# One PSUM pool for layers 0 and 1, and a pool of its own for layer 1's transposed x

## The chip, the core and the metric

The kernel runs on one core of a Trainium2 chip. The metric is the device time of one execution in microseconds, the median of three runs. The engines are TensorE (PE in the profile, PEld for its weight loads), VectorE (DVE), ScalarE (ACT), GpSimd (POOL) and SyncE (SP, which here only issues DMA transfers). All data are float32.

## The reference

Four residual layers act on x of 64 sequences, 32 positions and 512 features, so 2048 rows. Cut to the two layers that matter here:

```python
# layer 0: a weight per sequence, then a feed-forward part with a routed low-rank part and a layer norm
y = einsum('bsi,boi->bso', x, weight[ids])
h = relu(y @ up_w) ** 2
r = ((y @ fc1_w) @ expert_w) * sum(top_2(y @ gate_w))
x = x + layernorm(h @ down_w + r @ fc2_w) * gamma + beta

# layer 1: gated feed-forward part with a low-rank addition per sequence, then a weighted mix
gate = x @ W_gate.T + 0.5 * (x @ A_gate[ids].T) @ B_gate[ids].T      # 512 -> 1376
up   = x @ W_up.T   + 0.5 * (x @ A_up[ids].T)   @ B_up[ids].T
act  = silu(gate) * up
z    = act @ W_down.T + 0.5 * (act @ A_down[ids].T) @ B_down[ids].T  # 1376 -> 512
x = x + z @ W_base.T + b_base + mix_of_8_low_rank_experts(z)
```

Layer 2 is attention over a paged cache with a routed part behind it, and layer 3 a small mix per sequence with low-rank updates. The kernel runs layer 3 as a tail of layer 2.

## The kernel before

The 2048 rows are 16 tiles of 128. **Layer 0** (`layer0`) takes them in four groups of four tiles. For each group it forms y, transposes it, does the up-projection with a seven-product block scheme (`Up`, L251), and then for each tile (`Tile`) a choice (`choose`: L395, L397, L399), the down product `pd` in L246, and `last`: statistics of `pd` on VectorE (L417, L419, L421), a power on GpSimd (L130), the normalised z on VectorE (L424), times gamma on GpSimd (L425), plus x + beta (L426 on GpSimd, L427 on VectorE), and a store by SyncE (L428).

**Layer 1** (`layer1`) takes the tiles in eight groups of two. `Group.x` transposes two tiles of x on TensorE (L613, tile `xT_ps`) and copies them to `xT` on ScalarE (L614); `x_sums` forms four sums of its blocks on VectorE (L623 to L626); `low` is the first half of the low-rank part (`low_ps`). Then eleven blocks f of 128 features follow (`features`): gate and up together are one 2 x 2 block product, done with seven products `p1` to `p7` (all at L577, tiles `acc_a`, `acc_b`, `acc_c`) in place of eight. For this the weights must first be combined: `sums_of(f)` does four VectorE operations per block (L853 to L856), 44 in all, once, before the blocks of group 0 need them. `p1` and `p2` read the loaded weights alone; `p5`, `p6` and `p7` read sums, and `p4` a block of the up weights that the fourth operation has overwritten. `finish` adds the parts up on VectorE (L714, L738, L741 to L743, L747, L748). Behind a group's blocks stand `low_down` and `down`, and the choice and output of a group are done among the first blocks of the next. On the side GpSimd forms sums of the later layers' weights (`all_sums`, L493 to L496) from blocks that SyncE loads (L102), one set per block in the first blocks of each group.

The order: a scheduler orders the instructions of each engine when the program is built, by what they wait for in memory; only TensorE's order is written down by hand (`c.on_pe`), so that it is the program text's. DMA transfers of SyncE go in one queue (q1). A pool of SBUF or PSUM is a stretch of memory with tiles in it. Pools that are open at the same time lie one behind the other, and pools opened after others have closed lie over them; their tiles then wait for what the older pools still hold.

Layer 0's PSUM pool has eight banks under the tags tr, a, b, c, y0 to y3. Layer 1 opens another eight in its place: tr, lo, and two each of a, b and c. Its SBUF pools stand in this order: `l1_first_halves`, `l1_gathered0` and `1`, `l1_x`, `l1_gate_up` (gate1T, up1T and sums_gate_up, 75 KB of each partition), `l1_weights` (bias rows, cat1, base1T, B1), `l1_down`, `l1_group` (xT, x_sums, low_x, actT and others), `l1_tile`, `l1_sums`. Layer 0's are `l0_first`, `l0_seq_weights`, `l0_transposed_x`, `l0_up`, `l0_weights` (latent, down, fc2, gamma, beta), `l0_x`, `l0_group`, `l0_tile`.

Of the kernel before, what the change touches and what calls it, by code (L numbers as in the profile page):

```python
# [24 lines left out]
F32 = mybir.dt.float32  # L25
# [5 lines left out]
PSUM = bass.MemoryType.PSUM  # L31
DRAM = bass.MemoryType.DRAM

P = 128
B, S, D = 64, 32, 512
NT = B * S // P
SEQ = P // S
KC = D // P
# [109 lines left out]
        return call  # L148


def layer0(c, x_in, x_out):

# [1 line left out]
    tc, nc, a = c.tc, c.nc, c.a  # L156
    INT, LAT, NE = 1024, 256, 8
    G = 4
    N = G * P
    n_sets = a["cond0T"].shape[0]  # L160
    with ExitStack() as ctx:
# [6 lines left out]
        xp = ctx.enter_context(tc.tile_pool(name="l0_x", bufs=2))  # L168
        gp = ctx.enter_context(tc.tile_pool(name="l0_group", bufs=2))
        tp = ctx.enter_context(tc.tile_pool(name="l0_tile", bufs=2))  # L170
        ps = ctx.enter_context(tc.tile_pool(name="l0_psum", bufs=1, space=PSUM))

        def transposed_x(g, k, xT=None):
            if k is None:
# [266 lines left out]
        for g in range(groups):  # L441
            xT = transposed_x(g + 1, None) if 0 < g < groups - 1 else None
# [82 lines left out]
                         sums["out", h][:, k])  # L525


def layer1(c, kp, x_in, x_out, x_biased, sums):

# [2 lines left out]
    tc, nc, a = c.tc, c.nc, c.a  # L534
    G = 2
    N = G * P
# [3 lines left out]
    n_cat = NE * R + NE + 1  # L540
# [3 lines left out]
    with ExitStack() as ctx:  # L544
        rp = ctx.enter_context(tc.tile_pool(name="l1_first_halves", bufs=1))
        aps = [ctx.enter_context(tc.tile_pool(name=f"l1_gathered{i}", bufs=1)) for i in range(2)]
        xp = ctx.enter_context(tc.tile_pool(name="l1_x", bufs=4))
        gup = ctx.enter_context(tc.tile_pool(name="l1_gate_up", bufs=1))
        wp = ctx.enter_context(tc.tile_pool(name="l1_weights", bufs=1))
        wdp = ctx.enter_context(tc.tile_pool(name="l1_down", bufs=AHEAD))  # L550
        gp = ctx.enter_context(tc.tile_pool(name="l1_group", bufs=1))
        tp = ctx.enter_context(tc.tile_pool(name="l1_tile", bufs=2))
        sum_p = ctx.enter_context(tc.tile_pool(name="l1_sums", bufs=1))
        ps = ctx.enter_context(tc.tile_pool(name="l1_psum", bufs=1, space=PSUM))


        ids = c.load(kp, "ids1", [P, NT // G], a["ids1"], I32)
# [21 lines left out]
        class Group:  # L579
# [27 lines left out]

            def x(self, t, tag="tr"):
                if t == 0:
                    self.xT = gp.tile([P, KC, N], F32, name="xT")  # L610
                pt = ps.tile([P, KC, P], F32, tag=tag, name="xT_ps")
                for k in range(KC):
                    c.on_pe(nc.tensor.transpose(pt[:, k, :], self.xs[t][:, k * P:(k + 1) * P], c.ident))  # L613
                nc.scalar.copy(self.xT[:, :, t * P:(t + 1) * P], pt)  # L614
                nc.gpsimd.tensor_tensor(self.xs[t], self.xs[t], bias, ALU.add)
# [22 lines left out]

            def low(self):
                n = N // SEQ  # L640
                pt = ps.tile([P, 2, n], F32, tag="lo", name="low_ps")
                for u in range(2):
                    for k in range(KC):
                        for j in range(SEQ):
                            q = slice(2 * R * j, 2 * R * (j + 1))
                            product(pt[q, u, :], self.pair("x", u * KC + k, j),
                                    self.xT[:, k, j * n:(j + 1) * n], k == 0, k == KC - 1)
                self.low_x = gp.tile([P, 2, P], F32, name="low_x")
                self.masked(self.low_x, pt, own_half)

            def low_down(self):
                n = N // SEQ
                pt = ps.tile([P, 1, n], F32, tag="c", bufs=2, name="low_d_ps")
                for f, (_, w) in enumerate(FC):
                    for j in range(SEQ):
                        q = slice(2 * R * j, 2 * R * (j + 1))
                        product(pt[q, 0, :], self.pair("down", f, j)[:w],
                                self.actT[:w, f, j * n:(j + 1) * n], f == 0, f == NFC - 1)
                self.low_d = gp.tile([P, 1, N], F32, name="low_d")
                self.masked(self.low_d, pt, own)  # L660
# [8 lines left out]
            def begin(self, f):  # L669

                if f == 0:
                    self.actT = gp.tile([P, NFC, N], F32, name="actT")
                self.a[f] = ps.tile([P, D], F32, tag="a", bufs=2, name="acc_a")
                self.b[f] = ps.tile([P, D], F32, tag="b", bufs=2, name="acc_b")
                self.c[f] = ps.tile([P, D], F32, tag="c", bufs=2, name="acc_c")
                self.part[f] = {}

            def kept(self, f, name, src):
# [78 lines left out]

            def down(self, fs, last):
                if 0 in fs:
                    self.pz = [ps.tile([P, 2, N], F32, tag=tag, bufs=2, name="pz") for tag in "ab"]  # L760
                for f in fs:
                    w, wd = FC[f][1], self.wd.pop(0)
                    for m in range(KC):
                        product(self.pz[m // 2][:, m % 2, :], wd[:w, m * P:(m + 1) * P],
                                self.actT[:w, f, :], m % 2 == 0 and f == 0, False)
                    self.next_down(f + AHEAD)
                if not last:
                    return
                for m in range(KC):
                    product(self.pz[m // 2][:, m % 2, :], self.B["Bd1"][:, m * P:(m + 1) * P],  # L770
                            self.low_d[:, 0, :], False, m % 2 == 1)
                self.zT = gp.tile([P, KC, N], F32, name="zT")
                nc.scalar.copy(self.zT[:, 0:2, :], self.pz[0])
                nc.vector.tensor_copy(self.zT[:, 2:4, :], self.pz[1])

            def choose(self, t):

                q = slice(t * P, (t + 1) * P)
                ph = ps.tile([P, n_cat], F32, tag="lo", name="ph")
                for k in range(KC):  # L780
                    product(ph, self.zT[:, k, q], wcat[:, k, :], k == 0, k == KC - 1)
                h = tp.tile([P, n_cat], F32, name="h")
                nc.scalar.copy(h, ph)
                logits = h[:, NE * R:NE * R + NE]
                nm = tp.tile([P, 1], F32, name="nm")
                nc.vector.tensor_reduce(nm, logits, AX.X, ALU.max, negate=True)
                e = tp.tile([P, NE], F32, name="e")
                den = tp.tile([P, 2], F32, name="den")
                nc.scalar.activation(e, logits, AF.Exp, bias=nm, accum_out=den[:, 0:1])
                nc.scalar.activation(den[:, 1:2], h[:, n_cat - 1:n_cat], AF.Exp, bias=nb_thr,  # L790
                                     scale=-1.0)
                self.h[t] = h, e, den
# [17 lines left out]
                                        e.unsqueeze(2).to_broadcast([P, NE, R]), ALU.mult)  # L810

            def base(self, t, tag="tr"):
                self.po[t] = ps.tile([P, D], F32, tag=tag, bufs=2 if tag == "a" else 1, name="po")
                for k in range(KC):
                    product(self.po[t], self.zT[:, k, t * P:(t + 1) * P], wbase[:, k, :], k == 0, False)

            def turn(self, t):
                pt = ps.tile([P, P], F32, tag="lo", name="hwT_ps")
                c.on_pe(nc.tensor.transpose(pt, self.h[t].rearrange("p e r -> p (e r)"), c.ident))
                self.h[t] = tp.tile([P, P], F32, name="hwT")  # L820
                nc.scalar.copy(self.h[t], pt)
# [1190 lines left out]
def emit(tc, a, layers=(0, 1, 2)):  # L2012
    with ExitStack() as ctx:
        c = Common(ctx, tc, a)
        dram = ctx.enter_context(tc.tile_pool(name="scratch", bufs=1, space=DRAM))

        def scratch(name):
            tiles = [dram.tile([P, D], F32, name=f"{name}_{t}") for t in range(NT)]
            return lambda t: tiles[t]

        def rows(name):
            return lambda t: a[name][t * P:(t + 1) * P, :]

        x = rows("x")
        for n in layers:
            out = rows("out") if n == layers[-1] else scratch(f"x{n}")
            if n == 0:
                layer0(c, x, out)
            if n != 0 and n == next(m for m in layers if m):
                kp = ctx.enter_context(tc.tile_pool(name="known", bufs=1))  # L2030
                last = Tail(c)
                last.numbers(kp)
                known = Known(c, kp)
                sums = {}
                for h in range(HALVES):
                    sums["in", h] = dram.tile([P, GB, 4, KC // 2, D], F32, name=f"in_sums{h}")
                    sums["out", h] = dram.tile([P, HQP // 2, 4, D // 2], F32, name=f"out_sums{h}")
            if n == 1:
                x_biased = scratch("x_biased")
                layer1(c, kp, x, out, x_biased, sums)  # L2040
            elif n == 2:
                y_part, y = scratch("y_part"), scratch("y")
                attention(c, known, x, y_part, y, sums, last.between(x_biased, y, out))
            x = out
# [87 lines left out]
```

## Time and profile before

| | |
|---|---|
| median of three runs | 3472.89 us (3469.66 to 3475.73) |
| the profiled execution | 3470.0 us, span 3468.2 us from first to last instruction |
| granted TensorE clock, mean | 0.996 |
| busy: PE, DVE, ACT, POOL | 98%, 63%, 47%, 48% of the span |
| layer 0's last product on TensorE ends | 358.26 us |
| layer 1's first product begins | 361.04 us |
| PE busy from 300 to 450 us | 143.94 of 150 us |

How to read the lines: in a timeline the columns are start, duration (of a merged row: of the stretch), engine, line of the kernel, operation, tile written and tiles read, shapes, count, and in brackets the idle time before it with what ended it. In a list of waits they are the total, the number of waits and the longest. In the windows each engine's busy time stands with its number of instructions, then the granted TensorE clock as a share of full speed, the busy share of the DMA engines, and GB/s. A TensorE product in float32 is shown as two matmul records.

### The profile page before, as it was taken

How to read it: one execution, taken by the hardware profiler on the slowest of the kernel's cores; microseconds unless marked ns; L12 is line 12 of the kernel's file. 1: busy time of each engine (PE TensorE's matmuls, PEld its weight loads, DVE VectorE, ACT ScalarE, POOL GpSimd, SP SyncE). 2: the span in 40 equal slices, each digit the busy share in tenths (PEclk: the TensorE clock that was granted, in tenths of full speed). 3: DMA queues.
4: the chain of work that ended last, by engine and by line, in shares of the span. 5: the costliest groups of instructions: out<-in, count | busy, mean ns of one | idle time of the engine just before them, and what ended most of it. 6: DMA issues, size and time to landing. Idle time of an engine off the chain costs nothing. (4 is left out here: it accounts for less than half of the span.)

```text
span 3468.2 us, 66995 instructions
## 1 busy us (share of the span) xinstructions
PE 3412.8 (98%) x21124; PEld 2681.2 (77%) x21124; DVE 2189.0 (63%) x5429; ACT 1627.3 (47%) x4259; POOL 1653.6 (48%) x1650
## 2 busy tenths in 40 slices
PE   8999999999999999999999999999999999999999
PEld 6556788888857778777787777777877778778778
DVE  5454434334458677766767667677676776767467
ACT  6332222222226555555555555555555555656422
POOL 0112433333346655645556455565564655645233
PEclk9999999999999999999999999999999999999999
DMA  5013555545466788887888888878778888887731
GB/s 210 25 52 125 185 161 169 166 158 164 143 219 213 237 264 253 258 261 249 255 257 255 257 257 259 260 250 269 249 255 265 256 269 258 259 255 236 228 114 62
DMA packets 631937, 740.28 MB, mean 213 GB/s; under 512 B 64546, under 2 KB 480290, under 8 KB 631586
## 3 DMA queue, kind: packets, MB, share of 16 engines
q1 hardware_dynamic: 580130, 562.94, 52.1%
q0 software_dynamic: 51456, 173.05, 14.3%
q8 instruction: 172, 2.82, 0.3%
q14 instruction: 179, 1.47, 0.1%
HBM read 689.61 MB, written 46.14 MB: 212 GB/s over the span
## 5 line engine op out<-in xcount | busy, mean ns | idle before, releaser
L1086 POOL DMA_INDIRECT vt<-in_v_rows,v_rows x512 | 516.8, 1009 | 301.3 <-PE po L1060 176.1
L1349 ACT ACTIVATE pr<-pr,low 128x544 f32<-128x544 f32 x512 | 383.3, 749 | 548.0 <-DVE low L1347 546.0
L1342 PE MATMUL sc<-kt,qT 128*128 128x288 f32 (+1 forms) x2048 | 555.3, 394 | 9.1 <-DVE low L1347 5.9
L1342 PEld LDWEIGHTS sc<-kt,qT 128*128 128x128 f32 x2048 | 384.8, 190 | 224.3 <-issue 121.5
L1060 PEld LDWEIGHTS po<-prT,vt 128*128 128x128 f32 x4096 | 523.0, 192 | 33.4 <-ACT prT L1360 13.9
L1060 PE MATMUL po<-prT,vt 128*128 128x128 f32 x4096 | 544.7, 276 | 3.4 <-ACT prT L1360 1.9
L1347 DVE CUSTOM_DVE_ANT_0 pr<-sc,mask 128x544 f32<-128x544 f32 x512 | 368.1, 719 | 141.2 <-PE sc L1342 140.6
L1134 POOL TENSOR_TENSOR projected<-projected,swapped 128x512 f32<-128x512 f32 x160 | 208.3, 1302 | 302.1 <-DVE projected L1133 278.2
L1354 DVE TENSOR_SCALAR pr<-pr,low 128x512 f32<-128x512 f32 x512 | 317.8, 621 | 12.8
L1055 PE MATMUL prT_ps<-ident,pr 128*128 128x128 f32 x2048 | 312.1, 275 | 1.5 <-DVE pr L1354 1.3
L1360 ACT COPY prT<-prT_ps 128x512 f32<-128x512 f32 x512 | 294.0, 574 | 32.3 <-PE prT_ps L1055 24.7
L1351 DVE RECIPROCAL low<-low 128x1 f32<-128x1 f32 x512 | 81.9, 160 | 318.4 <-ACT pr L1349 317.7
L1055 PEld LDWEIGHTS prT_ps<-ident,pr 128*128 128x128 f32 x2048 | 237.7, 142 | 10.8 <-issue 2.8
L1060 PE MATMUL py<-wo,oT 128*128 128x256 f32 x1024 | 242.8, 380 | 0.0
L1060 PE MATMUL pq<-wp,x_sums 128*128 128x512 f32 x512 | 240.5, 593 | 0.1
L1060 PEld LDWEIGHTS py<-wo,oT 128*128 128x128 f32 x1024 | 187.4, 191 | 21.5
L130 POOL TENSOR_TENSOR rs<-rs,minus_half 128x4 f32<-128x4 f32 x160 | 180.1, 1125 | 22.2 <-DVE low L1351 14.6
L1060 PE MATMUL pq<-wp,xT 128*128 128x512 f32 x384 | 182.4, 598 | 5.0 <-DVE projected L1220 5.0
L1352 ACT ACTIVATE own_pr<-pr,low 128x32 f32<-128x32 f32 x512 | 164.8, 322 | 44.1 <-DVE low L1351 41.0
L1060 PE MATMUL py<-wo,o_sum 128*128 128x256 f32 x768 | 182.7, 382 | 2.1 <-DVE o_sum L1278 2.1
L1093 ACT COPY own_vt<-v 32x128 f32<-32x128 f32 x512 | 150.8, 295 | 55.1 <-PE po L1060 42.4
L1135 POOL TENSOR_TENSOR projected<-projected,rs 128x512 f32<-128x512 f32 x160 | 172.3, 1077 | 7.9
(348 smaller groups left out, 6459.4 us busy)
## 6 DMA issues: line engine op xcount, KB each, us to landing
kt<-in_kT SPq DMA_DIRECT2D x2048, 64.0 KB
wp<-in_sums SPq DMA_DIRECT2D x192, 512.0 KB
wo<-out_sums SPq DMA_DIRECT2D x128, 512.0 KB
wp<-in_WqT SPq DMA_DIRECT2D x96, 512.0 KB
wo<-in_WoT SPq DMA_DIRECT2D x96, 512.0 KB
down1T<-in_down1T SPq DMA_DIRECT2D x80, 256.0 KB
wp<-in_WkT SPq DMA_DIRECT2D x32, 512.0 KB
xt<-x SPq DMA_DIRECT2D x48, 256.0 KB
```

The costliest lines, as they stand in the source:

```text
L130: self.nc.gpsimd.tensor_tensor(t, t, self.minus_half[:, :n], ALU.pow)
L1055: c.on_pe(nc.tensor.transpose(pt[:, m, :], piece, c.ident))
L1060: c.on_pe(nc.tensor.matmul(out, lhsT, rhs, start=first and i == 0, stop=last and i == len(pairs) - 1))
L1086: nc.gpsimd.indirect_dma_start(out=vts[b % 2][:, n, :], out_offset=None, in_=a["v_rows"], in_offset=bass.IndirectOffsetOnAxis(ap=rows[h][: ...
L1134: nc.gpsimd.tensor_tensor(src, src, tmp, ALU.add)
L1135: nc.gpsimd.tensor_tensor(src, src, rs.unsqueeze(2).to_broadcast([P, REP, HD]), ALU.mult)
L1342: c.on_pe(nc.tensor.matmul(sc[:, lo + n * PSIZE:lo + m * PSIZE].rearrange("p (n k) -> p n k", k=PSIZE), q, kt[:, n:m, g, :], start=True, s ...
L1347: nc.vector.tensor_tensor_reduce(pr[:, :NK], sc[:, lo:lo + NK], masks[h, b], -SCALE, 3.0e38, ALU.add, ALU.min, low[:, 0:1])
L1349: nc.scalar.activation(pr[:, :NK], pr[:, :NK], AF.Exp, bias=low[:, 0:1], scale=-1.0, accum_out=low[:, 1:2])
L1352: nc.scalar.activation(own_prs[b % 2][:, g * S:(g + 1) * S], pr[:, L:NK], AF.Copy, scale=low[:, 2:3])
L1354: nc.vector.tensor_scalar(pr[:, :L], pr[:, :L], low[:, 2:3], None, ALU.mult)
L1360: last_prT.append(nc.scalar.copy(prT, pt).ins)
```

## The change

Layer 0 and layer 1 get one PSUM pool, opened before layer 0 and closed after layer 1. Layer 1 uses layer 0's tags: its tr keeps tr, lo takes c, and its pairs a, b and c take turns over a and y0, y1 and b, y3 and y2. In SBUF layer 1's `xT` leaves `l1_group` for a pool of its own of 4096 bytes per partition, which is opened between `l1_x` and `l1_gate_up`.

```diff
-def layer0(c, x_in, x_out):
+def layer0(c, ps, x_in, x_out):
...
-        ps = ctx.enter_context(tc.tile_pool(name="l0_psum", bufs=1, space=PSUM))
...
-def layer1(c, kp, x_in, x_out, x_biased, sums):
+def layer1(c, ps, kp, x_in, x_out, x_biased, sums):
...
         xp = ctx.enter_context(tc.tile_pool(name="l1_x", bufs=4))
+        xtp = ctx.enter_context(tc.tile_pool(name="l1_transposed_x", bufs=1))
         gup = ctx.enter_context(tc.tile_pool(name="l1_gate_up", bufs=1))
...
-        ps = ctx.enter_context(tc.tile_pool(name="l1_psum", bufs=1, space=PSUM))
+        places = {"tr": ("tr",), "lo": ("c",), "a": ("a", "y0"), "b": ("y1", "b"), "c": ("y3", "y2")}
+        turns = dict.fromkeys(places, 0)
+
+        def bank(shape, tag, name):
+            turns[tag] += 1
+            return ps.tile(shape, F32, tag=places[tag][(turns[tag] - 1) % len(places[tag])], name=name)
...
             def x(self, t, tag="tr"):
                 if t == 0:
-                    self.xT = gp.tile([P, KC, N], F32, name="xT")
-                pt = ps.tile([P, KC, P], F32, tag=tag, name="xT_ps")
+                    self.xT = xtp.tile([P, KC, N], F32, name="xT")
+                pt = bank([P, KC, P], tag, "xT_ps")
...
-                self.a[f] = ps.tile([P, D], F32, tag="a", bufs=2, name="acc_a")
-                self.b[f] = ps.tile([P, D], F32, tag="b", bufs=2, name="acc_b")
-                self.c[f] = ps.tile([P, D], F32, tag="c", bufs=2, name="acc_c")
+                self.a[f] = bank([P, D], "a", "acc_a")
+                self.b[f] = bank([P, D], "b", "acc_b")
+                self.c[f] = bank([P, D], "c", "acc_c")
...
+        banks = ExitStack()
+        ps = banks.enter_context(tc.tile_pool(name="l01_psum", bufs=1, space=PSUM))
         x = rows("x")
...
-                layer0(c, x, out)
+                layer0(c, ps, x, out)
...
-                layer1(c, kp, x, out, x_biased, sums)
+                layer1(c, ps, kp, x, out, x_biased, sums)
+                banks.close()
```

The other PSUM tiles of layer 1 (`low_ps`, `low_d_ps`, `pz`, `ph`, `po`, `hwT_ps`) go through `bank` in the same way.

More of the change, by code (lines that the diff above doesn't have):

```diff
@@ L640, in low @@
                 n = N // SEQ
-                pt = ps.tile([P, 2, n], F32, tag="lo", name="low_ps")
+                pt = bank([P, 2, n], "lo", "low_ps")
                 for u in range(2):
@@ L652, in low_down @@
                 n = N // SEQ
-                pt = ps.tile([P, 1, n], F32, tag="c", bufs=2, name="low_d_ps")
+                pt = bank([P, 1, n], "c", "low_d_ps")
                 for f, (_, w) in enumerate(FC):
@@ L759, in down @@
                 if 0 in fs:
-                    self.pz = [ps.tile([P, 2, N], F32, tag=tag, bufs=2, name="pz") for tag in "ab"]
+                    self.pz = [bank([P, 2, N], tag, "pz") for tag in "ab"]
                 for f in fs:
@@ L778, in choose @@
                 q = slice(t * P, (t + 1) * P)
-                ph = ps.tile([P, n_cat], F32, tag="lo", name="ph")
+                ph = bank([P, n_cat], "lo", "ph")
                 for k in range(KC):
@@ L812, in base @@
             def base(self, t, tag="tr"):
-                self.po[t] = ps.tile([P, D], F32, tag=tag, bufs=2 if tag == "a" else 1, name="po")
+                self.po[t] = bank([P, D], tag, "po")
                 for k in range(KC):
@@ L817, in turn @@
             def turn(self, t):
-                pt = ps.tile([P, P], F32, tag="lo", name="hwT_ps")
+                pt = bank([P, P], "lo", "hwT_ps")
                 c.on_pe(nc.tensor.transpose(pt, self.h[t].rearrange("p e r -> p (e r)"), c.ident))
```

## The prediction

> **What bounds the kernel now.** I read the page first (engines, chain), then what TensorE waited for around the end of layer 0, then that place instruction by instruction on PE, SyncE, VectorE and GpSimd, and last the windows with clock and DMA.
>
> ```profile
> PE 3412.8 (98%) x21124; PEld 2681.2 (77%) x21124; DVE 2189.0 (63%) x5429; ACT 1627.3 (47%) x4259; POOL 1653.6 (48%) x1650
> ```
>
> TensorE is busy for 3412.8 of 3468.2 us, so a delay of TensorE goes into the time unless a later wait absorbs it. What it waited for from 300 to 450 us, and its instructions there:
>
> ```profile
> PE xT_ps L613 <- issue: 2.8, 1, 2.8
> PE low_ps L577 <- ACT xT L614: 2.2, 1, 2.2
> ...
> 356.38 1.88 PE L246 MATMUL pd<-fc,eT 128*128 128x512 f32 x4
> 361.04 1.06 PE L613 MATMUL xT_ps<-ident,xt 128*128 128x128 f32 x8 [2.78 <-issue]
> 364.29 2.01 PE L577 MATMUL low_ps<-xT,first_x 128*32 128x64 f32 x64 [2.19 <-ACT xT L614]
> 366.23 1.22 PE L577 MATMUL acc_a<-xT,gate1T 128*128 128x128 f32 x4
> 367.24 1.06 PE L577 MATMUL acc_c<-x_sums,sums_gate_up 128*128 128x128 f32 x4
> ```
>
> Here layer 0 ends (358.26) and layer 1 begins. The two gaps, 2.78 and 2.19 us, are all that the change's words aim at: the first ends with VectorE's last read of a layer 0 bank (z L424, to 360.93), the second with the copy of layer 1's xT, held until layer 0's last z L427 (363.01). The line at 367.24 is the first to need a gate/up sum. Where the weights come from, on SyncE, GpSimd and VectorE:
>
> ```profile
> 315.95 0.38 SPq L87 DMA_DIRECT2D gate1T<-in_gate1T  x1
> 316.38 0.50 SPq L87 DMA_DIRECT2D up1T<-in_up1T  x1
> 357.67 0.33 SPq L428 DMA_DIRECT2D x<-z  x1
> 362.31 0.33 SPq L87 DMA_DIRECT2D bias_row<-in_bias  x1
> 361.01 1.27 POOL L425 TENSOR_TENSOR z<-z,gamma_row 128x512 f32<-128x512 f32 x1 [0.92 <-DVE z L424]
> 332.95 0.42 DVE L853 TENSOR_TENSOR sums_gate_up<-up1T,gate1T 128x256 f32<-128x256 f32 x1
> 375.16 0.81 DVE L747 SCALAR_TENSOR_TENSOR sg<-sg,gate 128x256 f32<-128x256 f32 x1 [1.44 <-ACT sg L746]
> 379.03 0.43 DVE L747 SCALAR_TENSOR_TENSOR sg<-sg,gate 128x256 f32<-128x256 f32 x1 [0.29 <-ACT sg L746]
> ```
>
> The weights are issued at 315.95, some 40 us before layer 0 ends, and their 44 sums (L853 to L856) run on VectorE from 332.95 to 357.03, under layer 0's matmuls. The bias row goes out only at 362.31: its place lies over layer 0's last weights, and it waits for the gamma multiplication of the last tile, which ends at 361.01 + 1.27 = 362.28. Of the windows:
>
> ```profile
> 318.00:320.00 2.00, 2.00 (x6) 0.92 (x5) 0.11 (x1) 0.50 (x2) 0.00 (x0) 1.00 0.97 385
> 330.00:332.00 2.00, 2.00 (x6) 0.80 (x6) 0.81 (x1) 0.00 (x0) 1.07 (x2) 1.00 0.62 253
> 364.00:366.00 2.00, 1.71 (x64) 1.71 (x64) 1.52 (x4) 0.24 (x1) 0.00 (x0) 0.50 0.97 273
> 368.00:370.00 2.00, 2.00 (x14) 2.00 (x14) 0.00 (x0) 0.50 (x2) 0.52 (x1) 0.67 0.98 326
> ```
>
> The last three columns are PE clock, DMA share, GB/s. The load of 2 x 2752 KB takes from 315.95 to about 331.5, at 385 to 427 GB/s once it runs. After the gaps the clock stands at 0.50 and is back at 1.00 only about 369.2, 4.9 us after PE restarts at 364.29.
>
> **The change part by part.** *The memory.* Layer 1's pools lie one behind the other over layer 0's. Before, gate and up weights and their sums (bytes 66,912 to 143,968 of each partition in the built program) end just short of layer 0's weight pool (from 144,832: latent, down, fc2, gamma, beta). So their load waited only for the last up-projection matmul, as its issue at 315.95 shows. xT's own pool of 4096 bytes goes in front and pushes them to 71,008 to 148,064: their last 3,232 bytes now lie over that pool, and the whole pool of gate and up waits until the whole pool under it has had its last reader, the gamma multiplication. The built order of the changed program says the same: gate1T's load stands behind the store of tile 14, waits for PE and GpSimd, and up1T's stands behind the store of tile 15; all 44 sums stand behind layer 0's last z on VectorE, 16 in a row and 28 strewn among the first features' operations. Matmuls and all other instructions stay in their order; none is added.
>
> *The load.* gate1T's issue: 315.95 to 362.31, the bias row's own moment under the same wait. Issue to landing as before: 331.5 - 315.95 = 15.5 us; the 256 KB store between the two loads, in the same queue, at about 400 GB/s: 0.7 us. up1T has landed at 362.31 + 15.5 + 0.7 = 378.5. The first sum takes 0.42, so PE's first product with a sum moves from 367.24 to about 379.0: **+11.8 us**. If the queue lets the 2 MB of bias, cat1, base1T and B1 loads that follow share its bandwidth, up1T lands up to 5 us later (2 MB at 400 GB/s); base1T (1 MB, issued 364.65) held up SyncE's wait until 372.5 while the rows ahead of it had gone first, so I take first come, first served, and keep the 5 us for the range.
>
> *What is gained.* The transposes can run at 358.3, the copies (0.53 each) at once, low_ps by about 362: both gaps close, worth 2.78 + 2.19 - 0.6 = 4.4 us, if anything followed. Nothing does: p1 needs gate1T (about 371), p5 the sums (379.0). PE stands for some 16 us instead of 5. Gain taken: 0, already inside the 11.8.
>
> *The clock.* Before, three blocks from 367.24 (0.86, 0.85 and 0.62 us) were slow against a pace of 0.445: 1.0 us lost. After, PE restarts cold at 379.0; 4.9 us at half clock lose 2.4. **+1.4 us**; ends 0 (the p1 block at 371 keeps the clock up for a while) and +2 (it takes longer after a longer rest). The Trainium skill, TensorE: Matmul & The Clock Gate, Part 1 on the clock gate, gives about 3.4 us of steady work until full rate; by that estimate the loss after would be 1.7, and the term +0.7. The row's 4.9 us is this kernel's.
>
> *VectorE in the first features.* A pair of features takes PE 7.55 us (VectorE's L714 comes back at 380.06 and 387.61). VectorE's own work in it is 9 operations at 0.29 and 4 at 0.43, 4.3 us, so 3.2 us are free. The changed order puts 28 sums into the first two pairs, 14 x 0.335 (their pitch in a row, 332.95 to 333.28 and on) = 4.7 us each: 1.5 us too much per pair, 3.0 in all. Besides, operations with both inputs in SBUF run slow beside GpSimd's block sums: sg took 0.81 at 375.16 with GpSimd adding, 0.43 at 379.03 without, +0.4 each. GpSimd does about two block sums of 4 adds (0.72 to 0.91 us each) in those 16 us: about 8 meetings x 0.4 = 3.2 us. PE's double accumulators give back about a microsecond. **+5 us**; ends: +1 (a whole feature of 3.8 us can be buffered; a gain is excluded, since the work is only added) and +9 (each of the 28 sums meets GpSimd: 28 x 0.4 = 11, less 2). I take the middle since the two rows it rests on are the same engines at the same place. The rule in the Trainium skill, SBUF — State Buffer, Who interferes with whom, speaks against this change: a VectorE operation with two SBUF inputs and a GpSimd operation that reads SBUF exclude each other, the later one blocked for the whole of the first. By it a meeting could cost up to 0.7 to 0.9 us, an add's whole length, and the term would be about +8.
>
> *At nothing.* The bias adds (L615, 366.03) move to about 380, their first reader is layer 1's first output, behind group 1's first features, past 430. cat1, base1T, B1 land by about 386 and are first read past 430 as well. b_thr's scaling on VectorE stands in the first feature and its row lands last, about 385, when VectorE gets there about 387: nothing, or 1 us if the rows are slow. first_down goes out about 11 us later than 378.99, needed at 430.8. The store wait of the first ACT copy ends under up1T's load. Shared PSUM banks keep two turns per accumulator: no difference once layer 1 runs.
>
> *Sum:* 11.8 + 1.4 + 5 = 18.2 us. PE waits only 3.0 us from 430 to 1000, and its later waits (sc on VectorE, pq on projected) hang on chains that start from PE itself, so nothing absorbs it. The profiled execution of before took 3470.0 (span 3468.2 and 1.8 around it); its like after is 3488.2. The median of the runs, 3472.9, becomes **3491**.
>
> **The rivals.** *Sums keep ahead* (VectorE term near +1, or the meetings rare): 11.8 + 1.4 + 1 = +14, 3487. For it: double accumulators; against: 4.7 us of sums into 3.2 us. *A shared queue*: up1T 5 us later and the sums colliding more: +26, 3499. For it: DMA falls to 143 GB/s between 366 and 368, so small-row loads can be slow. *Faster, the gaps close:* if the weights still went out at 316, PE would win 4.4 us, and without the gaps the clock would not fall (2.4 us before: 364.29 to 369.2 at half): -6.8, 3466. It decides if the load's wait ends before about 345 (15.5 us of load and 16 x 0.335 of sums ahead of 367); but it waits for a multiplication that ended at 362.28. *No change:* a later wait swallows the delay; the one long enough together (8.9 us of PE idle from 1000 to 1100) hangs on VectorE's projected and is itself moved.
>
> **How the numbers follow.** Forecast with VectorE at +3 to +8: 0.60. Sums keep ahead: 0.20. Shared queue: 0.14. No change: 0.03. Faster: 0.03. 0.2% of 3473 is 7 us, about what a measurement of this kernel tells from no change; so slower 0.94, same 0.03, faster 0.03. The range takes the first two rivals' neighbours: 3473 + 10 to 3473 + 27, 3483 to 3500.
>
> **What would show it.** Right: gate1T issued near 362, up1T after the last store, L853's counterpart first at 378 to 380, PE with two waits of about 9 and 7 us, clock 0.5 until about 384, PE waits on VectorE's up in the first four features, block sums on GpSimd some 11 us later, everything past 460 alike but 18 us late. Wrong: gate1T issued near 316; or sums that start near 379 and a PE delay that shrinks further on.

## The result and the profile after

The changed kernel takes 3495.87 us (median of 6 runs, 3491.13 to 3499.19) against 3475.07 us for the kernel before (6 runs), a ratio of 1.0058 with an interval of 1.0047 to 1.0069: 20.8 us slower, where +18.2 us and 3491 us were forecast. The profiled execution after was the longest of its six, 3499.2 us, and that of before near its lowest, 3470.0. They differ by 29.2 us; the last but one point of the section on the prediction says how much of that belongs to the change.

Where TensorE waited from 300 to 460 us, after (us in total, times, longest):

```profile
PE acc_a L582 <- DMA gate1T<-in_gate1T: 10.8, 1, 10.8
PE acc_c L582 <- DVE sums_gate_up L858: 6.4, 1, 6.4
PE acc_a L582 <- DVE up L719: 3.6, 5, 1.1
PE acc_a L582 <- DVE up L747: 0.8, 1, 0.8
PE low_ps L582 <- ACT xT L619: 0.7, 1, 0.7
...
```

In the kernel before the same list has one short wait for VectorE's `up`:

```profile
PE acc_a L577 <- DVE up L714: 0.5, 1, 0.5
```

The gap of 2.8 us ahead of layer 1's transposes is gone and the 2.2 us ahead of `low_ps` are 0.7: what the change's words aim at did come about. In its place stand 17 us of waiting for the gate and up weights and their first sum, and then for VectorE. SyncE's timeline shows from when, and TensorE's until when:

```profile
360.56 0.38 SPq L87 DMA_DIRECT2D gate1T<-in_gate1T  x1
361.83 0.76 SPq L87 DMA_DIRECT2D up1T<-in_up1T  x1
```

```profile
370.38 1.19 PE L582 MATMUL acc_a<-xT,gate1T 128*128 128x128 f32 x4 [10.80 <-DMA gate1T<-in_gate1T]
377.94 1.22 PE L582 MATMUL acc_c<-x_sums,sums_gate_up 128*128 128x128 f32 x4 [6.36 <-DVE sums_gate_up L858]
```

The loads of 315.95 and 316.38 now go out at 360.56 and 361.83, behind layer 0's last gamma product; the first product with a sum stands at 377.94 instead of 367.24. Layer 0 ended 1.9 us earlier in this execution (356.40 against 358.26), so the times here lie some 2 us early. VectorE's timeline behind the landing, with GpSimd's addition of the bias row:

```profile
377.46 0.43 DVE L858 TENSOR_TENSOR sums_gate_up<-up1T,gate1T 128x256 f32<-128x256 f32 x1 [15.04 <-DMA up1T<-in_up1T]
...
378.47 1.49 DVE L858 TENSOR_TENSOR sums_gate_up<-up1T,gate1T 128x256 f32<-128x256 f32 x1
379.88 1.48 DVE L861 TENSOR_TENSOR up1T<-gate1T,sums_gate_up 128x256 f32<-128x256 f32 x1
...
384.98 0.28 DVE L719 TENSOR_TENSOR up<-acc_a,p 128x128 f32<-128x128 f32 x1
378.24 2.84 POOL L620 TENSOR_TENSOR xt<-xt,bias_row 128x512 f32<-128x512 f32 x2 [17.71 <-DMA bias_row<-in_bias]
```

The first sum starts as up1T has landed. Two of its fellows take 1.49 and 1.48 us instead of 0.41, while GpSimd adds the bias row (L620, 378.24 to 381.08), and VectorE comes to the first feature's `up` only behind 16 sums, at 384.98. The kernel before already shows this price in layer 0, where a sum meets GpSimd's gamma product:

```profile
342.45 1.38 POOL L425 TENSOR_TENSOR z<-z,gamma_row 128x512 f32<-128x512 f32 x1 [0.92 <-DVE z L424]
342.62 1.49 DVE L855 TENSOR_TENSOR sums_gate_up<-up1T,sums_gate_up 128x256 f32<-128x256 f32 x1
```

Windows (each engine's busy time, last columns clock, DMA share, GB/s):

```profile
366.00:368.00 2.00, 0.00 (x0) 0.00 (x0) 0.00 (x0) 0.00 (x0) 0.00 (x0) 0.50 1.01 416
382.00:384.00 2.00, 2.00 (x15) 2.00 (x14) 2.00 (x8) 0.48 (x2) 0.00 (x0) 0.74 1.07 373
```

No engine works at 366 to 368 us, the DMA engines run full, and the clock is down; it comes back near 383.

### The profile page after: what moved, and what is told of

The parts are those of the page before. It is cut to its first block, busy times and chain, and to the rows that moved or that the text cites. A ratio compares the mean times of both kernels' runs of the same rounds, so it can differ in the third digit from the quotient of the medians.

```text
span 3497.4 us, 66991 instructions
## 1 busy us (share of the span) xinstructions
PE 3417.3 (98%) x21124; PEld 2681.9 (77%) x21124; DVE 2188.6 (63%) x5429; ACT 1626.9 (47%) x4259; POOL 1644.5 (47%) x1650
## 5 line engine op out<-in xcount | busy, mean ns | idle before, releaser
L130 POOL TENSOR_TENSOR rs<-rs,minus_half 128x4 f32<-128x4 f32 x160 | 180.1, 1126 | 22.6 <-DVE low L1356 14.9
```

The source lines that it names most:

```text
L130: self.nc.gpsimd.tensor_tensor(t, t, self.minus_half[:, :n], ALU.pow)
```

## The experiments

Single executions of one kernel scatter by several microseconds, so beside each ratio stands the **shift at the seam**, read from the traces. TensorE's matmuls come in the same order in every kernel, so they can be numbered. Two traces are laid together at the matmul that starts at 343.9 us in before, in layer 0. The shift is how much later than in before the matmul starts that stands at 413.3 us there, in layer 1's first group; a negative shift is a lead. For the changed kernel it is +19.5 us. Each shift comes from one execution; the three kernels that push the weights over the border and do nothing about it (the changed one, and e2 and e6 below) give 19.5, 19.3 and 19.1.

**The two halves of the change.** e1 is the changed kernel with xT back in `l1_group` (shared banks alone); e2 is the kernel before with the pool for xT in front of the weights (own banks).

```diff
e1, against the changed kernel
-        xtp = ctx.enter_context(tc.tile_pool(name="l1_transposed_x", bufs=1))
-                    self.xT = xtp.tile([P, KC, N], F32, name="xT")
+                    self.xT = gp.tile([P, KC, N], F32, name="xT")
e2, against the kernel before: the same lines the other way round
```

> The changed kernel with xT back in l1_group: only the PSUM pool is shared. Theory (the 4096 bytes in front of the gate and up weights push them over layer 0's last weights, and the wait for these is the whole loss): gate1T is issued near 316 us as before; the transposes follow layer 0's last product at once, but the copy of xT still waits for layer 0's last z, so low_ps begins where it did; the two gaps become one of about 5 us, and the time is that of before, 0 to -2 us. Rival (the shared banks and their turns cost something): slower than before by several us, up to the changed kernel's 21.

> The kernel before with xT in a pool of its own in front of the gate and up weights, PSUM pools as before. Theory: gate1T is issued only after GpSimd's last gamma multiplication, near 362 us, and the whole loss is here, +18 to +22 us. Rival (the loss comes from the shared banks): the time of before.

e1: 3474.36 us, ratio 0.9996 (0.9987 to 1.0006), shift +0.3. The transposes went early, at 357.82, and the list of TensorE's waits shows where the gain stayed:

```profile
PE low_ps L581 <- ACT xT L618: 5.1, 1, 5.1
```

The two gaps of before, 2.8 and 2.2, became one of 5.1: the copy of xT still waited for layer 0's last z. e2: 3492.77 us, ratio 1.0043 (1.0028 to 1.0059), shift +19.3; by the medians that is 17.6 us, just short of the 18 to 22 expected. The loss is the pool in SBUF alone; the banks bring nothing by themselves and cost nothing.

**How far the weights may be pushed.** e5 and e6 put an unused tile in front of the weights in the kernel before, below and above the 864 bytes that lie free between their end (143,968) and layer 0's weight pool (144,832).

```diff
+        gap = ctx.enter_context(tc.tile_pool(name="l1_gap", bufs=1)).tile([P, 128], F32, name="gap")
+        nc.gpsimd.memset(gap[:, 0:1], 0.0)
         gup = ctx.enter_context(tc.tile_pool(name="l1_gate_up", bufs=1))
(e6: [P, 256])
```

> The kernel before with an unused pool of 512 bytes in each partition opened in front of the gate and up weights. Their end moves from byte 143,968 to 144,480, still below 144,832, where layer 0's weight pool begins. Theory (the loss comes from the overlap with that pool alone): gate1T's load is issued as early as before, and the time is that of the kernel before, ratio 0.999 to 1.001. Rival (any displacement of the weights costs, in proportion to the bytes): 512 of 4,096 bytes, an eighth of e2's loss of 17.6 us, +2.2 us, ratio 1.0006.

> The kernel before with an unused pool of 1,024 bytes in each partition in front of the gate and up weights. Their end moves to 144,992, which is 160 bytes into layer 0's weight pool. Theory (a pool waits as a whole for the whole of what it touches): the entire loss of e2, which pushed by 4,096 bytes, comes at once: gate1T's load is issued behind layer 0's last tile, near 360 us, and the time is 3491 to 3495 us, ratio 1.004 to 1.006. Rival (only the tile that overlaps waits, sums_gate_up, which is made and not loaded; or the loss goes by bytes): gate1T comes early, +0 to +5 us, ratio 1.000 to 1.0015.

e5: 3477.96 us, ratio 1.0007 (0.9998 to 1.0016), shift -0.3. e6: 3494.49 us, ratio 1.0058 (1.0042 to 1.0073), shift +19.1. SyncE's timeline of e5, then of e6:

```profile
315.17 0.38 SPq L87 DMA_DIRECT2D gate1T<-in_gate1T  x1
```

```profile
361.98 0.38 SPq L87 DMA_DIRECT2D gate1T<-in_gate1T  x1
```

An overlap of 160 bytes moves the load by 46 us and costs as much as the change's 3,232; a push by 512 bytes, which ends short of the border, costs nothing that the seam shows (e5's ratio by itself can't exclude the rival's +2.2 us; its early load and its shift do). The wait is all or nothing, by pools: gate1T, whose own bytes lie far in front, waits as well.

**The weights' landing.** e8 is the changed kernel with both loads in four pieces, in turn.

```diff
-        wg, wu = c.chunks(gup, "gate1T"), c.chunks(gup, "up1T")
+        wg, wu = [gup.tile([P, KC, F1], F32, name=n) for n in ("gate1T", "up1T")]
+        for o, e in ((0, 256), (256, 640), (640, 1024), (1024, F1)):
+            for w, n in ((wg, "gate1T"), (wu, "up1T")):
+                nc.sync.dma_start(w[:, :, o:e], a[n].rearrange("(k p) n -> p k n", p=P)[:, :, o:e])
```

> The changed kernel, with gate1T and up1T loaded in four pieces of columns each (0 to 256, 256 to 640, 640 to 1024, 1024 to 1376), a piece of gate1T and a piece of up1T in turn, on the same queue and behind the same wait. Theory (of the loss, 12 us are the 5.6 MB that must land before the first sum, not the wait for the pool itself): the first product with a sum comes near 367 to 369 us instead of 377.9, TensorE no longer stands 10.8 and 6.4 us in one piece, and the time is 3484 to 3489 us against 3495.9 for the changed kernel; the pieces behind may add small waits of up to 3 us. Rival (the transfers of a queue share the engines, so that all pieces land about together, or the sums' order needs the last piece anyway): no gain, 3493 to 3498.

3485.25 us, ratio to before 1.0033 (1.0021 to 1.0045), shift +8.6. TensorE's timeline:

```profile
366.49 1.19 PE L582 MATMUL acc_a<-xT,gate1T 128*128 128x128 f32 x4 [5.34 <-DMA gate1T<-in_gate1T]
369.32 1.22 PE L582 MATMUL acc_c<-x_sums,sums_gate_up 128*128 128x128 f32 x4 [1.64 <-DVE sums_gate_up L861]
```

Under the same wait (gate1T's first piece goes out at 362.13) the first product with a sum comes 7.2 us after that issue instead of 17.4, and 10.9 of the 19.5 us are back (at that product the shift is 2.4 instead of 12.6; the rest of the 8.6 comes in the first features). The bytes ahead of the first sum were the larger part of the loss, as the sum had it.

**VectorE's part.** e7 is the changed kernel without block sums in group 0 (the other seven groups do them).

```diff
-            parts = [f for _ in range(5) for f in next(to_sum)]
+            parts = [f for _ in range((0, 6, 6, 6, 6, 6, 5, 5)[g]) for f in next(to_sum)]
```

> The changed kernel without the block sums of layer 2's weights in layer 1's first group of tiles (they are made in the seven groups behind it, six or five in each instead of five), so that VectorE and GpSimd have less beside the late sums of the gate and up weights. Theory (of the loss, some 5 us are VectorE's late sums, which stretch beside GpSimd's work and hold up the first features): TensorE's waits for VectorE's up fall from 3.6 us to under 2, and the time is 2 to 4 us below that of the changed kernel, 3492 to 3494 us. Rival (VectorE is late by its own queue of sums, whatever GpSimd does): the waits stay, 3495 to 3497 us.

3492.74 us, ratio to before 1.0052 (1.0037 to 1.0068), which overlaps the changed kernel's interval; the seam tells them apart, +16.4 against +19.5. Of TensorE's waits:

```profile
PE acc_a L582 <- DVE up L719: 1.7, 3, 0.9
```

3.6 us became 1.7, and the one wait for L747 is gone. So 3.1 us of VectorE's part come with the block sums. That it is by meetings the rows of VectorE support: from 384 to 416 us seven of its operations take longer than alone in the changed kernel, 2.8 us in all, and none in e7. (e7 leaves out the block sums' loads in that group as well.)

**Can the gaps be closed for gain?** e3 and e4 make room by moving `first_down` (5,632 bytes) behind `l1_down`, so that gate and up end at 142,432, short of layer 0's weights. Both keep xT's own pool in front; e3 has the change's shared banks, e4 own ones.

```diff
+        fdp = ctx.enter_context(tc.tile_pool(name="l1_first_down", bufs=1))
...
-                t = rp.tile([P, NS * R, src.shape[2] // R], F32, name="first_" + what)
+                t = (rp if what == "x" else fdp).tile([P, NS * R, src.shape[2] // R], F32, name="first_" + what)
```

> The changed kernel with first_down (5632 bytes) taken out of l1_first_halves to a pool behind l1_down, so that gate and up weights and their sums end at byte 142,432, short of layer 0's weight pool at 144,832. Theory: gate1T is issued near 316 again, the sums run under layer 0, and now both gaps close: -4 to -7 us against before (the gaps 2.78 and 2.19 less 0.6, and up to 2.4 of slow clock). Rival (xT in front or the shared banks cost something of their own): no gain or slower than before.

> As the run before, but with layer 0's and layer 1's own PSUM pools. Theory: the transposes begin only after VectorE's last read of layer 0's banks (gap of 2.8 us stays), the copy of xT follows them at once, so low_ps begins about 1.6 us earlier than before: -1 to -3 us, and the rest of the gain of the run before belongs to the shared banks. Rival (xT's place alone is enough): the same gain as the run before.

e4: 3473.74 us, 0.9992 (0.9983 to 1.0001), shift -0.8, no difference that the medians tell. e3 missed: 3476.37 us, 1.0001 (0.9992 to 1.0010), shift +0.7. Its loss was gone, but not a microsecond was won. Its timelines, first TensorE, then ScalarE:

```profile
361.68 0.61 PE L583 MATMUL acc_b<-xT,gate1T 128*128 128x128 f32 x4
366.47 1.22 PE L583 MATMUL acc_a<-x_sums,sums_gate_up 128*128 128x128 f32 x4 [4.18 <-ACT p L687]
```

```profile
366.15 0.27 ACT L687 COPY p<-acc_a 128x128 f32<-128x128 f32 x1 [7.04 <-DMA x<-z]
```

Both gaps are closed and the weights are there: up to the first of these two lines e3 leads by 5.7 us. `p1`, the first tile of `l1_tile`, lies in a pool that reaches over `l0_tile`, whose last user is the store of layer 0's last z, issued at 362.6. The copy waits until 366.15, TensorE stands 4.18 us for the bank, and its clock, still 1.00 in the window from 362 to 364, is at 0.50 from 366 to 370: the lead is gone. In the kernel before that store is issued at 363.04, but there the copy stands behind the two gaps and starts at 367.53, as soon as TensorE's product is there, so the store costs nothing.

e9 is e3 with `l1_tile` opened ahead of `l1_group`; e10 besides gives x_sums and low_x a pool in front of both; e11 is e10 with own banks.

```diff
+        xsp = ctx.enter_context(tc.tile_pool(name="l1_x_sums", bufs=1))      (e10, e11)
+        tp = ctx.enter_context(tc.tile_pool(name="l1_tile", bufs=2))
         gp = ctx.enter_context(tc.tile_pool(name="l1_group", bufs=1))
-        tp = ctx.enter_context(tc.tile_pool(name="l1_tile", bufs=2))
...
-                s = gp.tile([P, 4, K2, P], F32, name="x_sums")
+                s = xsp.tile([P, 4, K2, P], F32, name="x_sums")      (e10, e11; low_x alike)
```

> This is e3 (the changed kernel with first_down in a pool behind l1_down) with one more edit: layer 1's pool of work tiles, l1_tile, is opened ahead of l1_group, so that it no longer lies over layer 0's pool of the same kind. In e3 the gap closed as forecast (layer 1's transposes began at 357.4 us instead of 361.0), but ScalarE's first copy p1 out of acc_a then waited until 366.15 for layer 0's last store (x<-z, issued at 362.6), TensorE stood 4.2 us behind it, and its clock fell to 0.50 again: 6.5 us of lead at the fourth product were all gone two features later. Theory (a new wait took the place of the old one, and it is the placing of this pool that makes it): p1's wait is gone, the lead of 5 to 6.5 us stays, and the time is 3468.5 to 3471 us against 3475 for the kernel before (ratio 0.998 to 0.999). Rival (yet another wait takes its place, GpSimd's bias add, the second features' copy or a later stage): the ratio is 0.9995 to 1.0005, as for e3, and the list of TensorE's waits between 300 and 460 us shows which.

e9 missed as well: 3478.14 us, 1.0010 (1.0001 to 1.0019), shift +1.1. The list of TensorE's waits and VectorE's timeline:

```profile
PE acc_c L583 <- DVE x_sums L629: 5.4, 1, 5.4
```

```profile
366.22 0.80 DVE L629 TENSOR_TENSOR x_sums<-xT 128x256 f32<-128x256 f32 x1 [3.55 <-DMA x<-z]
```

The swap had put `l1_group` over `l0_tile`, and x_sums with it: the same store, another tile that waits for it.

> e9 missed: p1 no longer waited, but l1_group had moved over layer 0's tile pool instead, and with it x_sums, so that VectorE's block sums of x waited for the same last store and TensorE stood 5.4 us for them. Here x_sums and low_x get a pool of their own, opened ahead of l1_tile, and l1_group, which now holds what is first written some 10 us later (actT, low_d, zT), stands behind it: nothing that layer 1 needs before 366 us lies over layer 0's x tiles or its tile pool any more. Theory (each early tile over that pool waits for the last store, and nothing else stands there): TensorE runs through from the transposes to the first features, with waits of under 2 us in all, its clock stays at 1.00, the lead over the kernel before is 5 to 7 us at 400 us, and the time is 3468 to 3471 us (ratio 0.998 to 0.999). Rival (a third wait, such as VectorE's x_sums beside GpSimd's product, or the lead is lost again between 1,000 and 1,200 us, where the kernels with shared banks and an own pool for xT have lost 2 to 4 us): ratio 0.9990 to 1.0005.

> The pools of e10, but each layer with its own pool of PSUM banks as in the kernel before. Theory (the shared banks close the 2.8 us that TensorE stands ahead of layer 1's transposes, and only where nothing behind waits longer): that gap is back, the clock falls for some 5 us behind it, and the lead over the kernel before is 1 to 3 us at 400 us, so 3 to 5 us less than in e10; time 3472 to 3474.5 us. Rival (the shared banks are worth nothing even with the way clear): the same lead as e10 within 1 us.

e10's forecast missed; of e11's the gap and the lead at 400 us came (2.4), the time did not. e10: 3473.97 us, 0.9995 (0.9986 to 1.0004), shift -2.6. e11: 3476.24 us, 1.0004 (0.9995 to 1.0013), shift -1.2. The way is clear in e10: the clock stands at 1.00 in every window from 356 to 384 us, and at the matmul that before starts at 368.1 it leads by 5.8 us, e11 by 1.7. Of its waits:

```profile
PE acc_a L584 <- DVE up L721: 1.3, 3, 0.5
PE acc_a L584 <- DVE up L749: 1.1, 1, 1.1
```

3.2 us of e10's lead are gone at 413.3: most of it shows as these waits, VectorE being late where TensorE is early. What stays, 2.6 us by the seam, is below what the medians tell from no change. The shared banks are worth 4.1 us in front (5.8 against 1.7), but 0.8 at 400 us (3.2 against 2.4), where 3 to 5 were expected and the rival said less than 1, and 1.4 at the seam: e10 loses in the first features most of what it gains ahead of them. None of the versions beats the kernel before beyond its interval.

## Why the prediction was right

- **The mechanism** (weights pushed over layer 0's weight pool, the load as late as the bias row): right, by e2, e5 and e6. gate1T's issue went from 315.95 to 360.56, under the wait forecast; the 362.31 of the forecast is the same moment in an execution whose layer 0 ended 1.9 us later. One detail was wrong without cost: not all other instructions kept their order. Two of layer 1's four `x_sums` ran on VectorE ahead of layer 0's last z (at 358.99 and 359.32).
- **The load, +11.8:** the first product with a sum came at 377.94. TensorE was 1.9 us early in layer 0 (at 343.9), so that is 377.94 + 1.9 - 367.24 = 12.6. First come, first served held nearly: up1T was there 16.9 us after gate1T's issue (360.56 to 377.46), where the sum had 15.5 + 0.7 = 16.2 and a fair share for the 2 MB of later rows would have made it some 5 us more. The two waits were 10.8 and 6.4 for about 9 and 7.
- **The gaps, gain 0:** right. They closed and won nothing, since the sums came last.
- **The clock, +1.4:** the pitch of the products was about 0.85 us from 377.94 until about 383.0 and 0.445 behind, 5.1 us of half speed, where the row of before had 4.9. The shift grows from 12.6 at the first product with a sum to 14.1 where both traces are back at full pace (371.36 in before, 383.58 after): +1.5. The estimate by the Trainium skill, TensorE: Matmul & The Clock Gate, Part 1 (about 3.4 us), which would have given +0.7, is too short for this row.
- **VectorE, +5:** the rest of the shift, 19.5 - 14.1 = 5.4. Its part by meetings with block sums was put at 3.2 and is 3.1 by e7. The other 2.3 us agree with the sum (3.0 for the late sums, less 1 for the accumulators) partly by luck, for it had left something out. What was set at nothing and was not: the bias adds. They met two sums and stretched them from 0.41 to 1.49 and 1.48, 2.1 us of VectorE's row of 16. The price stood in the trace of before (1.49 at 342.62). TensorE's first wait for `up`, 1.11 us until 385.31, ends behind both stretched sums. Without their 2.1 us `up` would have been there before TensorE asked for it (an estimate from these rows); how much of the 2.1 us counts in the end was not measured apart. The rule of the Trainium skill, SBUF — State Buffer, Who interferes with whom, is closer for the bias adds (1.08 us more beside an add of about 1.4) than for the block sums, and its +8 is too much for the whole.
- **Nothing absorbs it:** right. The shift is 19.5 at 413 us and 20.1 at 978. Behind that single executions wander: 22.7 at 1,195 and 22.6 at 3,170. At the end it is 31.1, but between 3,170 and 3,438 us the traces of all eleven experiments, too, lose 0.7 to 6.9 us against the trace of before, whatever their edit (this one 8.5): that trace was quick there. The medians' 20.8 agree with the seam, not with the 29.2 of the two profiled executions. Whether the 2.6 us between 978 and 1,195 belong to the change stays open: e3 has them (3.3), and so has e5 (2.2), with the banks of before and the weights early; e1 (0.5) and e2 (-0.5, with the weights late) have not.
- **The rival that the gaps close, -6.8:** e3 took away its condition's obstacle, the late load, and got +0.7. The rival had missed that the first copy's wait for the last store, which the prediction rightly hid under up1T's load, is the next to end once that load is early. With that gone too (e10) the lead is 5.8 us in front, near the 6.8, and 2.6 behind the first features.

## What to carry to other kernels

In this kernel pools laid over older ones waited as wholes: before a small pool is put in front of a large one, compare the large one's new end with the next old pool's start, and ask who reads that old pool last; here 160 bytes of overlap cost as much as 3,232. What must be early in the new stage belongs over memory that falls free early, and the big load that nobody else hides is worth splitting in the order of its use. And a gap that closes is worth only the time to the next wait: list them all, here the copy of xT, the work tiles, the block sums, before a gain is counted.

## What the runs showed of the hardware

A VectorE add of 128x256 with both inputs in SBUF takes 0.41 us alone and up to 1.50 beside a GpSimd product or add over 512 columns: 1.48 and 1.49 in the changed kernel, 1.49 in e3, 1.48 in e9, 1.50 in e10. The granted clock fell some time after TensorE stopped. In e11 that was behind the gap: TensorE stood 2.8 us until 360.86 and, after the transposes, 0.8 more, the window from 360 to 362 still has 1.00, and those to 364 and 366 have 0.56 and 0.59. In the changed kernel's longer gap, from 359.6 to 370.38, it fell in it: 1.00 in the window to 362, 0.64 in that to 364. In e10, where the longest wait was 1.1 us, it stayed at 1.00. In e8 the first piece of gate1T could be used 4.4 us after it was sent (362.13 to 366.49), while seven more pieces were being issued behind it in the same queue until 371.67.
